# Attention of two pairs ahead of their feed-forward parts, the first pair's token factors put by in DRAM

## The chip, the cores and the metric

The kernel runs on one core of one Trainium2 chip. The metric is the device time of one execution in microseconds, which is shown as the median of several runs. Before the change it is 1606.5 us (three runs, 1605.66 to 1609.31).

## What is computed

The input `x` holds 8 sequences of 512 tokens with 512 features, all float32. Cut to what matters, the reference is:

```python
xn = _layernorm(x)
# s: linear attention
q, k, v = xn @ Wq.T + bq, xn @ Wk.T + bk, xn @ Wv.T + bv
kv_sum = cumsum((elu(k) + 1) * v, axis=1)          # over the tokens
s = ((elu(q) + 1) * kv_sum * SCALE) @ Wo.T + bo
# g: gated feed-forward with Hadamard transforms
h = fwht(xn * SU_ug) / SCALE_F
up = h @ W_up.T * (Wscale_ug[:2048] * SCALE_F)     # 2048 hidden features
gate = h @ W_gate.T * (Wscale_ug[2048:] * SCALE_F)
h = fwht(silu(gate) * up * SU_dp) / SCALE_F
g = silu(h @ W_down.T * (Wscale_dp * SCALE_F))
out = x + s * g
```

`fwht` is the normalized Walsh-Hadamard transform over the last axis. The products of tokens with the four attention weights and the three feed-forward weights are nearly all of the arithmetic.

## The kernel before, in words

The 8 sequences are worked on as four pairs, in a loop `for p in range(B // 2)` (line 935). A pair goes through attention (six groups of products: `k`, `v`, `q` for each half `g` of the features, line 529), the output projection (`project_out`, 601), four feed-forward units (`NU = 4`), and a down projection after the second and after the fourth unit (`down`, 703).

Every matrix product is made with seven block products in place of eight, called P1 to P7. For this, tokens and weights are held as seven factors each: four blocks and three sums or differences. The products are added up in four kinds of PSUM bank, `px` (three buffers), `py` (one), `pz` (two), and `t` (two, for transposes and folds). ScalarE copies a bank that has to be kept (`sa`, `sb`, `sc`, line 328), and VectorE adds the copy and another bank to an output block (line 332). TensorE can use a bank again only after it has been read. In attention and in the first pair's gate and up, `group` (306) makes such a product with matmuls of 128x512 (line 316).

The token factors of a pair are one tile `xo` of 128 partitions x 7 x 7 x 256 numbers, in a pool with one buffer (`xop`, line 64). Four of the second seven are needed by attention and by the first pair's gate and up. The other three are for the later pairs' feed-forward, which uses the seven-product scheme on two levels (49 products of 128x256, `hidden_unit` 647 and `block_product` 467, line 475). `inner_tokens` (157) makes them with three VectorE subtractions of 128x1792, and `inner_t3` (163) finishes with one subtraction for each of the seven outer factors.

The first pair differs from the others, since the weights arrive raw. The Hadamard transform is folded into the weights on the chip:

- Gate and up (`folded_w`, 748): four VectorE butterflies (759 to 762), two matmuls with the Hadamard matrix `had` (768), four scaled ScalarE copies (774), four VectorE sums that make the weight factors (`encode_weights`, 175). `inner_w` (253) then makes and stores the factors of the second level in DRAM, for the later pairs.
- Down (four column blocks `o`): `load_down` (788) brings 1 MB, `butterflies_down` (793) makes one scaling (795) and eight VectorE butterflies of 128x1024 (745, 746), `fold_down` (802) four matmuls (806), sixteen scaled ScalarE copies (812) and a store to `wd_f` (815). `down_w` (241) loads rows of `wd_f` into a `t8` buffer, makes weight factors on VectorE, and stores them.
- The projection weights' factors are made on GpSimd (835) and kept in DRAM (`keep_w`, 189).

The down weights' steps are set in time by a plan, which counts finished groups of products (`between`, 929) and gives the steps a priority of 150 behind what is current (`background`, 75):

```python
for o, (n, a, b) in enumerate(((0, 0, 2), (2, 4, 6), (4, 6, 8), (6, 8, 10))):   # load, butterflies, fold
for n, u, j in ((10, 0, 0), (10, 0, 1), (11, 1, 0), (11, 1, 1), (16, 2, 0), (17, 2, 1), (18, 3, 0), (19, 3, 1)):   # down_w
```

All weights pass through one list, `queue` (845). `get_w` (873) asks for the next three and sets the steps that make them; their loads go to SyncE's DMA queue (SP) in that order. The order of products within and across groups is an agenda (`at`, `advance`, 283 to 300). A scheduler then places all instructions on their engines by dependence and priority. Each engine works through its own list in order, so that an instruction that waits holds up all that stand behind it on its engine.

Other lines that are needed below: `load_x` (105), `layernorm` (116) and `transposed` (137) bring a sequence in. The two sequences of the next pair come through a pool with one buffer (`xin`, 67). In attention, ScalarE and VectorE make elu + 1 (549 to 551), GpSimd multiplies `v` by it (563), VectorE sums over the tokens with scans (565), and the context `co` is made by VectorE (573) and GpSimd (`encode_tokens`, 168). The hidden factors `ho` are made on GpSimd from gate and up (637 to 640). `put_by` and `fetch` (587, 592) keep the attention result `s_` and the first half `d_` of the down projection in DRAM; the second down projection fetches them and `x` again as `y` (976 to 981), and finishes with silu on ScalarE (710), a product on GpSimd (712), a sum on VectorE (713) and the store of the output (716).

The pools in SBUF: `hop` has two buffers of 28 KB a partition, which hold the raw `x` of the first two sequences, `co`, `ho`, and at first the down weights' work tile `rd` (917). `t8` has six of 8 KB, `wpool` four weights, `snap` six.

Of the kernel before, what the change touches and what calls it, by code (L numbers as in the profile page):

```python
# [21 lines left out]
def kernel(  # L22
# [41 lines left out]
    xop = ctx.enter_context(tc.tile_pool(name="xop", bufs=1))  # L64
    hop = ctx.enter_context(tc.tile_pool(name="hop", bufs=2))
# [70 lines left out]

    def transposed(b, xt, xo):
# [15 lines left out]
        if s == 1:  # L153
            o = xo[:, :, 0:4]
            nc.vector.tensor_tensor(o[:, P4], o[:, P2], o[:, P6], ALU.subtract)

    def inner_tokens(xo):

        nc.vector.tensor_tensor(xo[:, :, P5], xo[:, :, P7], xo[:, :, P1], ALU.subtract)
        nc.vector.tensor_tensor(xo[:, :, P6], xo[:, :, P3], xo[:, :, P5], ALU.subtract)  # L160
        nc.vector.tensor_tensor(xo[:, :, P4], xo[:, :, P2], xo[:, :, P6], ALU.subtract)

    def inner_t3(xo, factors):
        for i in factors:
            nc.vector.tensor_tensor(xo[:, i, P7], xo[:, i, P3], xo[:, i, P7], ALU.subtract)

# [300 lines left out]
    def block_product(name, w, x, out, add, done):  # L467
# [5 lines left out]
        def product(p, i, first):  # L473
            for lane in range(2):
                nc.tensor.matmul(  # L475
                    p[:, lane], w[:, lane, i, :], x[:, i, :],
# [52 lines left out]
    def attention(p, xo, get_w):  # L529
        co = hop.tile([P, 2, 7, L], F32, tag="h", name=f"co_{p}")  # L530

        def project(m, g, then):
# [11 lines left out]
            )  # L544

# [101 lines left out]
    def hidden_unit(p, u, xo, ho, get_w, last):  # L647
# [4 lines left out]
        def outer(i, out, add=None, done=None):  # L652
            w = get_w("gu", (u, i))
            block_product(f"gu_{p}_{u}_{i}", w, xo[:, i], out, add, done)
# [87 lines left out]
    def butterfly(eng, dst, src, h):  # L742
        s = src.rearrange("p (a t h) e -> p a t (h e)", t=2, h=h)
        d = dst.rearrange("p (a t h) e -> p a t (h e)", t=2, h=h)
# [42 lines left out]

    def load_down(o, rs):
        r = rs[:, o % 2]
# [3 lines left out]
    def butterflies_down(o, rs):  # L793
        r, r2 = rs[:, o % 2], rs[:, 2]
        nc.vector.tensor_tensor(r, r, wsc_r.unsqueeze(1).to_broadcast([P, NF, P]), ALU.mult)
        butterfly(nc.vector, r2, r, 8)
        butterfly(nc.vector, r, r2, 4)
        butterfly(nc.vector, r2, r, 2)
        butterfly(nc.vector, r, r2, 1)
# [46 lines left out]
    for p in range(B // 2):  # L846
        queue += [(p, m, g) for g in range(2) for m in ("k", "v", "q")]
        for u in range(NU):
            if p == 0:
                queue += [(p, m, f) for m in ("gate", "up") for f in (u, u + NU)]  # L850
            else:
                queue += [(p, "gu", (u, i)) for i in (P1, P5, P6, P2, P7, P3, P4)]
            if u == 0:
                at_o = len(queue) - (2 if p == 0 else 0)
                queue[at_o:at_o] = [(p, "o", 0), (p, "o", 1)]
            if u % 2:
                queue += [(p, "down", (u // 2, i)) for i in (P1, P7, P2, P6, P5, P3, P4)]
    ahead = []

    def ask(n):  # L860
        while queue and len(ahead) < n:
            p, m, g = queue.pop(0)
            w, steps = (first_w if p == 0 and m != "down" else later_w)(m, g)
# [9 lines left out]
    def get_w(m, g):  # L873
# [15 lines left out]
    xs = [  # L889
        load_x(b, hop.tile([P, 2, 7, D], F32, tag="h", name=f"x_{b}")[:, 0, :NT], parts=2)  # L890
        for b in range(2)
    ]
# [12 lines left out]
    xo = xop.tile([P, 7, 7, H], F32, tag="xo", name="xo_0")  # L905
    for b in range(2):
        layernorm(b, xs[b], parts=2)
        transposed(b, xs[b], xo)
# [8 lines left out]
    rs = hop.tile([P, 3, NF, P], F32, tag="h", name="rd")  # L917
    rd = {}
    groups = [0]

    plan = {}
    for o, (n, a, b) in enumerate(((0, 0, 2), (2, 4, 6), (4, 6, 8), (6, 8, 10))):
        plan.setdefault(n, []).append(lambda o=o: load_down(o, rs))
        plan.setdefault(a, []).append(lambda o=o: rd.update({o: butterflies_down(o, rs)}))
        plan.setdefault(b, []).insert(0, lambda o=o: fold_down(o, rd[o]))
    for n, u, j in ((10, 0, 0), (10, 0, 1), (11, 1, 0), (11, 1, 1), (16, 2, 0), (17, 2, 1), (18, 3, 0), (19, 3, 1)):
# [8 lines left out]
    for p in range(B // 2):  # L935
        if p:
            with background():
                inner_tokens(xo)
        co = attention(p, xo, get_w)
# [93 lines left out]
```

## Time and profile before

| | |
|---|---|
| median of three runs | 1606.5 us |
| the profiled execution | 1606.13 us |
| its span in the profile | 1604.3 us |
| granted TensorE clock | 0.992 |
| TensorE matmul (PE) busy | 1550.9 us, 97%, 5936 instructions |
| TensorE weight load (PEld) busy | 1117.1 us, 70% |
| VectorE (DVE) busy | 949.2 us, 59%, 1335 instructions |
| ScalarE (ACT) busy | 425.1 us, 26%, 679 instructions |
| GpSimd (POOL) busy | 504.9 us, 31%, 286 instructions |
| moved by DMA | 254.29 MB, 159 GB/s in the mean |
| chain of work that ended last | TensorE 73%, VectorE 12%, DMA 5%, "issue" 4%, GpSimd 3%, ScalarE 2% |

The page has more parts: the span in 40 equal slices of 40 us, each with the busy share of every engine in tenths; groups of instructions by source line; and the chain of work that ended last. The trace behind it can be asked for an engine's timeline, in which each row has the start, the length, the engine, the line, the operation with its output and inputs by the program's names, the shape of the tiles, and in square brackets the idle time of the engine before the row with the engine and the instruction that ended it. It can also be asked for tables of windows, with the busy time of each engine in a stretch and the number of instructions that make it up. Matmuls overlap, so that a busy TensorE can still be a slow one: the distance between the starts of equal matmuls tells its pace.

### The profile page before, as it was taken

What the parts mean: (1) busy time and instruction counts of PE and PEld (TensorE: products, weight loads), DVE (VectorE), ACT (ScalarE), POOL (GpSimd) and SP (SyncE); (2) the same over time, 40 slices, a digit from 0 to 9 for tenths busy, and PEclk for the clock granted to TensorE, in tenths of its full rate; (3) what the DMA queues carried; (4) which work ended last, traced back from release to release, by engine and by line L of the source; (5) the groups of instructions that cost most, each with busy time, mean ns of one, the idle gap of its engine ahead of it and who ended that gap; (6) DMA issues with size and microseconds to landing.
All of it is one profiled execution on the core that took longest, in us unless ns stands there. A gap on an engine that the chain in (4) does not pass through costs nothing.

```text
span 1604.3 us, 15681 instructions
## 1 busy us (share of the span) xinstructions
PE 1550.9 (97%) x5936; PEld 1117.1 (70%) x5936; DVE 949.2 (59%) x1335; ACT 425.1 (26%) x679; POOL 504.9 (31%) x286
## 2 busy tenths in 40 slices
PE   6979989999999999999999999999999999999998
PEld 3335435854485478888886478888887468888887
DVE  6869666268565574715675475634675466542673
ACT  3333322132324431111222531111221441111211
POOL 4531342103322235302622236201622137120731
PEclk9999999999999999999999999999999999999999
DMA  8234559397763244335574232535474224525472
GB/s 266 80 111 135 180 148 300 84 280 215 250 218 129 69 138 145 131 107 189 178 255 144 90 107 102 193 91 188 158 265 157 69 93 137 176 83 190 141 261 84
DMA packets 147723, 254.29 MB, mean 159 GB/s; under 512 B 7232, under 2 KB 109120, under 8 KB 143552
## 3 DMA queue, kind: packets, MB, share of 16 engines
q1 hardware_dynamic: 147360, 253.00, 47.9%
q8 instruction: 47, 0.77, 0.2%
q10 hardware_dynamic: 288, 0.30, 0.1%
q14 instruction: 28, 0.23, 0.0%
HBM read 183.53 MB, written 69.73 MB: 158 GB/s over the span
## 4 chain that ended last, share of the span: by engine, by line
PE 73%; DVE 12%; DMA 5%; issue 4%; POOL 3%; ACT 2%; SPq 1%; POOLq 0%; DVEq 0%; ACTq 0%
PE px_gu L475 18%; PE pz_gu L475 9%; PE px_dn L391 8%; PE py_gu L475 5%; PE pz_dn L391 4%; PE px_o L391 3%; PE px_v L316 3%; PE px_k L316 3%; PE px_q L316 3%; PE py_dn L391 2%; DMA x<-in_x_dram 2%; POOL s L712 2%; PE pz_o L391 2%; PE pz_q L316 2%; PE pz_k L316 1%
## 5 line engine op out<-in xcount | busy, mean ns | idle before, releaser
L475 PE MATMUL px_gu<-xo,w_gu 128*128 128x256 f32 x1344 | 320.6, 380 | 0.0
L475 PEld LDWEIGHTS px_gu<-xo,w_gu 128*128 128x128 f32 x1344 | 254.7, 190 | 39.9 <-issue 3.6
L391 PE MATMUL px_dn<-w_down,ho 128*128 128x256 f32 x1024 | 230.1, 379 | 2.2 <-DVE sb_dn L402 1.7
L391 PEld LDWEIGHTS px_dn<-w_down,ho 128*128 128x128 f32 x1024 | 193.6, 190 | 31.4 <-DVE sb_dn L402 2.7
L475 PE MATMUL pz_gu<-xo,w_gu 128*128 128x256 f32 x672 | 173.1, 380 | 0.0
L675 POOL TENSOR_TENSOR u<-u,v 128x1024 f32<-128x1024 f32 x24 | 56.1, 2360 | 354.2 <-DVE u L513 354.2
L475 PEld LDWEIGHTS pz_gu<-xo,w_gu 128*128 128x128 f32 x672 | 127.0, 190 | 19.1 <-DVE a L517 0.9
L391 PE MATMUL pz_dn<-w_down,ho 128*128 128x256 f32 x512 | 116.6, 380 | 1.9 <-POOL ho L172 1.9
L391 PEld LDWEIGHTS pz_dn<-w_down,ho 128*128 128x128 f32 x512 | 96.4, 190 | 17.6 <-POOL ho L172 2.7
L712 POOL TENSOR_TENSOR s<-s,d 128x512 f32<-128x512 f32 x30 | 43.0, 1435 | 166.2 <-ACT d L710 166.2
L475 PE MATMUL py_gu<-xo,w_gu 128*128 128x256 f32 x336 | 86.2, 379 | 0.0
L563 POOL TENSOR_TENSOR v<-v,k 128x1024 f32<-128x1024 f32 x16 | 39.8, 2486 | 138.5 <-ACT v L538 110.3
L637 POOL TENSOR_TENSOR ho<-g,u 128x512 f32<-128x512 f32 x8 | 17.8, 2224 | 186.0 <-DVE u L332 186.0
L475 PEld LDWEIGHTS py_gu<-xo,w_gu 128*128 128x128 f32 x336 | 63.9, 190 | 8.7
L316 PE MATMUL px_k<-xo,w_k 128*128 128x512 f32 x128 | 63.0, 616 | 3.7 <-ACT sa_k L328 3.4
L316 PE MATMUL px_up<-xo,w_up 128*128 128x512 f32 x128 | 60.4, 600 | 4.0 <-DVE w_up L178 4.0
L679 POOL TENSOR_TENSOR v<-v,r 128x1024 f32<-128x1024 f32 x24 | 56.2, 2364 | 25.6 <-DVE r L513 25.6
L316 PE MATMUL px_v<-xo,w_v 128*128 128x512 f32 x128 | 60.2, 593 | 3.5 <-ACT sc_v L328 3.5
L316 PE MATMUL px_q<-xo,w_q 128*128 128x512 f32 x128 | 60.2, 593 | 0.0
L316 PE MATMUL px_gate<-xo,w_gate 128*128 128x512 f32 x128 | 59.6, 593 | 0.0
L565 DVE TENSOR_TENSOR_SCAN k<-ones,v 128x512 f32<-128x512 f32 x32 | 39.4, 1271 | 33.5 <-POOL v L563 33.5
L391 PE MATMUL py_dn<-w_down,ho 128*128 128x256 f32 x256 | 58.0, 379 | 0.0
(241 smaller groups left out, 2469.0 us busy)
## 6 DMA issues: line engine op xcount, KB each, us to landing
w_gu<-d_gu SPq DMA_DIRECT2D x84, 896.0 KB, 4.5
w_down<-d_down SPq DMA_DIRECT2D x56, 512.0 KB, 3.6
d_s<-o SPq DMA_DIRECT2D x8, 1024.0 KB, 4.4
d_d<-dn SPq DMA_DIRECT2D x8, 1024.0 KB, 7.5
d<-d_d SPq DMA_DIRECT2D x8, 1024.0 KB, 6.2
s<-d_s SPq DMA_DIRECT2D x8, 1024.0 KB, 7.3
y<-in_x_dram SPq DMA_DIRECT2D x8, 1024.0 KB, 8.4
out_dram<-y SPq DMA_DIRECT2D x16, 512.0 KB, 3.1
```

Of the source, the lines that this page charges most:

```text
L316: nc.tensor.matmul(p.rearrange("p a t -> p (a t)") if len(r.shape) == 2 else p, ws[k][:, i, :], r, start=(first and k == 0), stop=(k == n ...
L391: nc.tensor.matmul(p[:, c], t[:, (2 * g + c) * P : (2 * g + c + 1) * P], ws[i](k), start=(first and k == 0 and c == 0), stop=(k == n - 1), ...
L475: nc.tensor.matmul(p[:, lane], w[:, lane, i, :], x[:, i, :], start=(first and lane == 0), stop=True, skip_group_check=True,)
L563: nc.gpsimd.tensor_tensor(v[:, h], v[:, h], k[:, h], ALU.mult)
L565: nc.vector.tensor_tensor_scan(k[:, h, s], ones.to_broadcast([P, L]), v[:, h, s], 0.0, ALU.mult, ALU.add)
L637: nc.gpsimd.tensor_tensor(ho[:, P1], g[:, 0, 0], r[:, 0, 0], ALU.mult)
L675: nc.gpsimd.tensor_tensor(r[:, m], ru1[:, m], rv[:, m], ALU.add)
L679: nc.gpsimd.tensor_tensor(rv[:, m], rv[:, m], rr[:, m], ALU.add)
L712: (nc.vector if last else nc.gpsimd).tensor_tensor(r, r, d, ALU.mult)
```

## The change

Pair 0's attention is followed by pair 1's attention. Then comes pair 1's feed-forward, then pair 0's. Pairs 2 and 3 run as before, each with its attention and its feed-forward.

- Token factors: the tile `xo` is split into `xo` (7 x 4 x 256, pool `xop`) and `xi` (the three inner ones, 7 x 3 x 256, new pool `xip` with one buffer). Pair 0's `x0` lies in a `hop` buffer; the raw `x` of sequences 0 and 1 lie in `t8` buffers.
- During pair 0's attention, after its first and third group, sequences 2 and 3 are loaded, normalized and transposed into pair 1's `x1`, with a priority of 40 behind what is current. After its second group, `put_x0` writes `x0` (128 x 7168 numbers, 3.67 MB) to DRAM.
- Pair 0's output projection runs after the first group of pair 1's attention; its weights stand there in the queue.
- Pair 1's feed-forward is now the one with raw weights. After its last unit, `fetch_x0` reads the 3.67 MB back into `xo` and makes the inner factors in `xi`. Pair 0's feed-forward uses the stored weight factors, as those of pairs 2 and 3.
- The down weights' work tile lies where `xi` will be. It holds two and a half column blocks in place of three, so that the butterflies run over halves of 64 columns: sixteen of half the size, in place of eight, for each block. The rearrangement in `butterfly` keeps two axes apart for that.
- The plan's numbers are set anew, since twelve groups of attention and the output projection now stand ahead of the first gate. Folds are put at the end of their step's list in place of its front.

The instructions of attention, feed-forward and down projection are otherwise those of before. The core of the diff:

```diff
+    xip = ctx.enter_context(tc.tile_pool(name="xip", bufs=1))
...
+    def new_x(p, pool):
+        return pool.tile([P, 7, 4, H], F32, tag="h" if pool is hop else "xo", name=f"xo_{p}")
+
+    def new_inner(p):
+        return xip.tile([P, 7, 3, H], F32, tag="xi", name=f"xi_{p}")
...
-    def inner_tokens(xo):
-
-        nc.vector.tensor_tensor(xo[:, :, P5], xo[:, :, P7], xo[:, :, P1], ALU.subtract)
-        nc.vector.tensor_tensor(xo[:, :, P6], xo[:, :, P3], xo[:, :, P5], ALU.subtract)
-        nc.vector.tensor_tensor(xo[:, :, P4], xo[:, :, P2], xo[:, :, P6], ALU.subtract)
+    def inner_tokens(xo, xi):
+
+        nc.vector.tensor_tensor(xi[:, :, P5 - P4], xo[:, :, P7], xo[:, :, P1], ALU.subtract)
+        nc.vector.tensor_tensor(xi[:, :, P6 - P4], xo[:, :, P3], xi[:, :, P5 - P4], ALU.subtract)
+        nc.vector.tensor_tensor(xi[:, :, 0], xo[:, :, P2], xi[:, :, P6 - P4], ALU.subtract)
...
+    def inner_factor(xo, xi, i):
+        return lambda k: xo[:, i, k] if k < P4 else xi[:, i, k - P4]
...
-    def attention(p, xo, get_w):
+    def attention(p, xo, get_w, behind):
+
+        n = iter(range(6))
...
+            behind.get(next(n), lambda: None)()
...
     def butterfly(eng, dst, src, h):
-        s = src.rearrange("p (a t h) e -> p a t (h e)", t=2, h=h)
-        d = dst.rearrange("p (a t h) e -> p a t (h e)", t=2, h=h)
+        s = src.rearrange("p (a t h) e -> p a t h e", t=2, h=h)
+        d = dst.rearrange("p (a t h) e -> p a t h e", t=2, h=h)
...
+    def down_tiles(rs):
+        n = NF * P
+        r = [rs[:, i * n : (i + 1) * n].rearrange("p (c e) -> p c e", c=NF) for i in range(2)]
+        return r + [rs[:, 2 * n : 2 * n + n // 2].rearrange("p (c e) -> p c e", c=NF)]
...
     def butterflies_down(o, rs):
-        r, r2 = rs[:, o % 2], rs[:, 2]
+        r, r2 = rs[o % 2], rs[2]
         nc.vector.tensor_tensor(r, r, wsc_r.unsqueeze(1).to_broadcast([P, NF, P]), ALU.mult)
-        butterfly(nc.vector, r2, r, 8)
-        butterfly(nc.vector, r, r2, 4)
-        butterfly(nc.vector, r2, r, 2)
-        butterfly(nc.vector, r, r2, 1)
+        for e in range(2):
+            half = r[:, :, e * P // 2 : (e + 1) * P // 2]
+            butterfly(nc.vector, r2, half, 8)
+            butterfly(nc.vector, half, r2, 4)
+            butterfly(nc.vector, r2, half, 2)
+            butterfly(nc.vector, half, r2, 1)
         return r
...
+    list_attention(True, 0)
+    list_attention(False, 1, [("o", 0), ("o", 1)])
+    queue[7:9] = [(True, "o", 0), (True, "o", 1)]
+    list_ffn(True, False, True)
+    list_ffn(False, False, False)
+    for p in range(2, B // 2):
+        list_attention(False, p)
+        list_ffn(False, False, True)
...
-    xs = [
-        load_x(b, hop.tile([P, 2, 7, D], F32, tag="h", name=f"x_{b}")[:, 0, :NT], parts=2)
-        for b in range(2)
-    ]
+    xs = [load_x(b, t8.tile([P, NT, D], F32, tag="t", name=f"x_{b}"), parts=2) for b in range(2)]
...
-    xo = xop.tile([P, 7, 7, H], F32, tag="xo", name="xo_0")
+    x0 = new_x(0, hop)
...
-    rs = hop.tile([P, 3, NF, P], F32, tag="h", name="rd")
+    rs = down_tiles(xip.tile([P, 7 * 3 * H], F32, tag="xi", name="rd"))
...
-    for o, (n, a, b) in enumerate(((0, 0, 2), (2, 4, 6), (4, 6, 8), (6, 8, 10))):
+    for o, (n, a, b) in enumerate(((0, 1, 3), (3, 5, 7), (6, 8, 10), (9, 11, 13))):
         plan.setdefault(n, []).append(lambda o=o: load_down(o, rs))
         plan.setdefault(a, []).append(lambda o=o: rd.update({o: butterflies_down(o, rs)}))
-        plan.setdefault(b, []).insert(0, lambda o=o: fold_down(o, rd[o]))
-    for n, u, j in ((10, 0, 0), (10, 0, 1), (11, 1, 0), (11, 1, 1), (16, 2, 0), (17, 2, 1), (18, 3, 0), (19, 3, 1)):
+        plan.setdefault(b, []).append(lambda o=o: fold_down(o, rd[o]))
+    for n, u, j in ((14, 0, 0), (15, 0, 1), (15, 1, 0), (16, 1, 1), (22, 2, 0), (23, 2, 1), (24, 3, 0), (25, 3, 1)):
         plan.setdefault(n, []).append(lambda u=u, j=j: down_w(u, j))
...
+    def tokens(b, xo):
+        t = load_x(b)
+        layernorm(b, t)
+        transposed(b, t, xo)
...
+    def load_next(p):
+        held["x"] = [load_x(2 * p + s) for s in range(2)]
+        for s in range(2):
+            layernorm(2 * p + s, held["x"][s])
+
+    def transpose_next(p):
+        held["xo"] = new_x(p, xop)
+        for s in range(2):
+            transposed(2 * p + s, held["x"][s], held["xo"])
...
+    def put_x0():
+        nc.sync.dma_start(d_x0, x0.rearrange("p i k t -> p (i k t)"))
+
+    def fetch_x0():
+        held["xo"] = xo = new_x(0, xop)
+        nc.sync.dma_start(xo.rearrange("p i k t -> p (i k t)"), d_x0)
+        held["xi"] = xi = new_inner(0)
+        with background():
+            inner_tokens(xo, xi)
+            inner_t3(xo, range(7))
+
+    x1 = new_x(1, xop)
+
+    def next_tokens(b):
+        with background(40):
+            tokens(b, x1)
+
+    co0 = attention(0, x0, get_w, {0: lambda: next_tokens(2), 1: put_x0, 2: lambda: next_tokens(3)})
+    co1 = attention(1, x1, get_w, {0: lambda: project_out(0, co0, get_w)})
+    ffn(1, x1, None, True, co1, {3: fetch_x0})
+    ffn(0, held["xo"], held["xi"], False, None, {2: lambda: load_next(2), 3: lambda: transpose_next(2)})
+    for p in range(2, B // 2):
+        xo, xi = held["xo"], new_inner(p)
+        with background():
+            inner_tokens(xo, xi)
+        co = attention(p, xo, get_w, {})
+        inner_t3(xo, (P1, P5, P6, P2, P7))
+        at(9, lambda: inner_t3(xo, (P3, P4)))
...
```

`ffn` holds what the loop over the pairs held (line 935 on): the four units, the output projection after the gates or after the first unit if there is one to do, the two down projections, and after each unit the step that it is given in `after`.

## The prediction

> **What bounds the kernel now.** I read the page's slices first, then TensorE's timeline for its gaps, then VectorE's timeline at those gaps. In the slices (40 us each, busy tenths) PE is short of 9 only in the first 240 us and near 480 us:
>
> ```profile
> PE   6979989999999999999999999999999999999998
> DVE  6869666268565574715675475634675466542673
> ```
>
> Busy PE is not PE at its peak, so I use its pace. In the timeline eight 128x512 records take 3.43 us and the 80 `px_dn` records of 128x256 take 17.27 us, so 0.429 and 0.216 us each. The later pairs run at that pace: their first `px_k` stand at 497.8, 868.9 and 1237.8 us, 369 to 371 us apart, and their records (168 x 0.429 for attention, 784 + 112 + 448 at 0.216 for the rest) make 362 us, with transposes some 366. The first pair takes 479 us from 18.4 to 497.8 us. Its records are 168 + 448 + 96 of 128x512 (attention, gate and up, folds), 305 us, and 560 of 128x256, 121 us, with transposes about 432: some 45 us are lost, and only there can this change gain. TensorE's timeline shows where; the bracket is the idle time before the row and what ended it:
>
> ```profile
> 63.27 3.00 PE L316 MATMUL pz_q<-xo,w_q 128*128 128x512 f32 x4 [3.55 <-DVE q L332]
> ...
> 89.84 1.96 PE L316 MATMUL px_v<-xo,w_v 128*128 128x512 f32 x4 [3.52 <-ACT sc_v L328]
> ...
> 106.66 3.78 PE L316 MATMUL pz_q<-xo,w_q 128*128 128x512 f32 x4 [4.32 <-DVE q L332]
> ...
> 150.74 2.00 PE L391 MATMUL pz_o<-w_o,co 128*128 128x256 f32 x8 [3.05 <-DVE g L332]
> ...
> 202.96 2.69 PE L316 MATMUL px_up<-xo,w_up 128*128 128x512 f32 x4 [4.02 <-DVE w_up L178]
> ...
> 228.34 3.47 PE L316 MATMUL pz_gate<-xo,w_gate 128*128 128x512 f32 x4 [3.62 <-DVE g L332]
> ...
> 497.77 3.58 PE L316 MATMUL px_k<-xo,w_k 128*128 128x512 f32 x4 [2.28 <-ACT sa_k L328]
> ```
>
> Four such rows usually take 1.88 us. After a gap[...] they take more, here and in the next row: 1.9 us at 63, 2.7 at 107, 1.8 at 203, 1.6 at 228. So the six waits of 63 to 228 us cost 5.4 + 3.5 + 7.0 + 3.1 + 5.8 + 5.2 = 30 us, and one of 1.3 us at 235 makes 31.3. VectorE's timeline shows what stands in front of the awaited result:
>
> ```profile
> 57.69 3.33 DVE L565 TENSOR_TENSOR_SCAN k<-ones,v 128x512 f32<-128x512 f32 x2 [2.24 <-POOL v L563]
> 60.94 1.68 DVE L745 TENSOR_TENSOR rd<-rd 128x1024 f32<-128x1024 f32 x1
> 62.54 0.67 DVE L332 TENSOR_TENSOR q<-sc_q,pz_q 128x512 f32<-128x512 f32 x1
> ```
>
> The 0.67 us sum that TensorE waits for lies behind two scans, which wait for POOL, and behind a down-weight butterfly. The windows say the same: VectorE is full at 60 to 100 us, and in the second pair's attention it isn't:
>
> ```profile
> 60.00:80.00 20.00, 16.49 (x34) 7.06 (x35) 20.00 (x18) 8.18 (x10) 7.88 (x5) 0.91 0.22 75
> ...
> 540.00:560.00 20.00, 20.00 (x48) 8.76 (x47) 10.04 (x12) 9.95 (x13) 6.20 (x5) 1.00 0.20 73
> ```
>
> (Columns: stretch, length, PE, PEld, DVE, ACT, POOL busy, clock, DMA share, GB/s.)
>
> [...]That is what the two windows show: one VectorE-bound, one with VectorE half idle. [...]the butterflies' median is 1220 ns, but 1393 (L745) and 1533 ns (L746) in the mean, longest where POOL works.
>
> **The change, part by part.**
>
> *Work.* Pair 1 takes over the raw gate and up products, pair 0 the stored seven-factor ones; records, folds and transposes only change places. TensorE's sum stays the same: 0 us.
>
> *Butterflies.* 32 instructions of 1024 elements become 64 of 512. [...]the trace has 1220 and 690. Started back to back they take 1.13 and 0.60 us in the timeline: 64 x 0.60 - 32 x 1.13 = +2.2 us of VectorE, up to +5 if the start isn't hidden. I take 0 on the path, as one pair's attention has some 40 us of free VectorE; without that cover it is 2 to 5 us. Shorter pieces also hold a waiting sum for less: up to -0.6 us a wait.
>
> *VectorE in the first attention.* It loses one set of butterflies and the gate folds (2.3 + 9.1 and about 5 us) and, by the built program's order, gets the layernorm and evacuation of sequences 2 and 3: 8 BN_STATS at 0.65, 8 scalings at 0.6, 12 subtractions at 0.4, one of 1.3 us, small ones: about 18 us. So the first attention is hardly lighter. The second has 37 us of its own and the output projection's 16 x 0.6 = 10, against 96 us of TensorE, and takes 2.5 butterfly sets at 12 us: 77 of 96 us. In the first feed-forward unit one set is left instead of two. So I count the waits at 63, 90, 107, 203, 228 and 235 us as gone (28 us) and keep 3 us for the one at 151.
>
> *New wait 1, transposes.* In the built order TensorE has sequence 2's transposes after the first half of the second `k` group, at 53.6 us on the old clock. They wait for VectorE: after the first scan (50.3, set by POOL's product) come statistics (2 us), a sum, three scans to about 59 us (POOL's second product takes from 54 to 57), then the scaling: 60 us. So 6.5 us, and 1.8 for the restart: 8 us; from 5[...] to 15 (loads late). Sequence 3 has one buffer with it and starts loading at about 63 us; its transposes come at 86: 1 us, up to 4.
>
> *Storing pair 0's factors.* 128 x 7168 x 4 B is 3.67 MB, put on SP's queue at about 27 us, in front of `w_v` (issued at 37.4 us in the old trace) and sequence 2's load. [...]the trace's best windows move 325 to 346 GB/s, so 11 to 13 us. It ends at about 40 us, as `w_v` is issued, and replaces 2 MB of down weights there. I take 0; at 200 GB/s it costs 6 us, which is in the 15 above. Hidden by attention's TensorE work.
>
> *New wait 2, output projection.* It now stands in the second pair's first `k`, with 20 half butterflies among its sums. VectorE reaches the last `co` product about 118 us when TensorE wants it at 114: 4 us, between 0 and 7. Three fold sets before the first gate leave TensorE waiting for ScalarE's scaled copies: four copies take 1.14 us against 0.43 of matmul, two banks: 2 us (0 to 4).
>
> *New wait 3, down weights.* Their encoding is asked for two to three groups earlier, its loads waiting on SP for a POOL-held `t8` buffer and standing on VectorE in front of `u`'s sums: 3 us, between 0 and 9.
>
> *The joint between the feed-forwards.* Old: 2.3 us at 497.8 with 1.7 us of restart, and some 2.5 us of small waits before. New: the 3.67 MB come back after the last up product of pair 1 (447 us on the old clock) and land some 13 us later; on SP `y` twice (2 MB) and then the fourth `w_down` stand behind. At 340 GB/s that weight lands 20 us after the up, and TensorE wants it after 16: 4 us and 1.7 of restart; with half a dozen small waits 7 us, so 0.5 more than before. Bounds: 0 and 18.
>
> **Sum.** Gone 28. New: 8 + 1 + 4 + 2 + 3 + 0.5 = 18.5. Net -9.5 us on the profiled execution's 1606.13 us (span 1604.3, 1.8 around it), which lies 0.4 under the median of 1606.5: 1597 us.
>
> **Rivals.**
> - B, new waits stay small. For it: the later pairs' attentions run the same products and scans without loss, once no butterflies stand between them. Against it: the first attention has layernorms there instead. The waits 1 to 3 then cost 8 instead of 18: 1587 us.
> - C, VectorE stays the limit: what is taken from one place is paid at another, as VectorE has the same work to do before the second feed-forward unit, only spread over 96 us more of TensorE. For it: the new waits 1 to 3 are all VectorE's; at two thirds of the way to their upper ends they make up for what went. Gone 28, new 27: 1605 us.
> - D, slower, by the fetch of pair 0's factors. VectorE runs in order; its seven-factor subtractions (3 x 2.0 us and 7 x 0.4 to 0.7) stand in front of the down sums that free TensorE's banks. If the fetch lands 13 us after the last up they end in time within 2 us. Each later microsecond is one of TensorE. It is slower than before once it lands 26 us after, as when the 2 MB of `y`, the 1 MB of `x` and the rest of `d` and `s` (3 MB) share the engines: 9.7 MB at 340 GB/s is 29 us, 1612 us with the restart. Against it: `d`, `s` and `x` are issued 12 us earlier.
> - That the change doesn't do what it says can't be: the built order has both attentions ahead of the first gate.
>
> **How the numbers follow.** Forecast 0.48 (1591 to 1602), B 0.20 (1580 to 1591), C 0.15 (1602 to 1609), D 0.17 (over 1609). A measurement of this kernel tells about 0.2%, 3.2 us, from no change. Faster by more: most of the forecast and B, a little of C, 0.70; within: 0.13; slower: 0.17. The range leaves out the lower third of B and two thirds of D: 1583 to 1612.
>
> **What would show it.** Right: no wait of 3 us on `pz_q` before the first gate, one of 5 to 9 us before sequence 2's transposes ended by VectorE's scaling, VectorE below 18 of 20 us in all windows of the second attention, no wait for `w_up`'s encoding in the first unit. Wrong: `px_dn` or `w_down` waits of over 8 us in pair 1's second down; waits for `u` or `w_gate` sums in the first unit above 8 us together; or transposes that don't wait at all.

## The result, and the profile after

The changed kernel takes 1607.99 us in the median (12 runs, 1602.70 to 1612.04), the kernel before 1605.69 us beside it (12 runs). The ratio is 1.0014 with a 95% interval of 0.9999 to 1.0028: no change that can be told, +2.2 us on 1605.7 where -9.5 was forecast. The profiled execution of the changed kernel took 1603.91 us (span 1602.1), one of the shorter ones of its kernel, and that of before 1606.13. So the two traces differ by 2 us the other way: they are used here for the places where time is lost, not for how much the kernels differ. The median execution of the changed kernel is 4 us longer than the profiled one, and no trace places these 4 us.

First the page's slices of the changed kernel, 40 us each, busy tenths:

```profile
PE   6888999899999999999999999999999999999998
DVE  5697867672576446715675575634675466542673
```

PE is short of 9 in the first four slices and at 280 to 320 us. The short slice of before at 200 to 240 us has filled up and the third has risen from 7 to 8, but the second and the fourth have sunk from 9 to 8, and VectorE has a 9 at 80 to 120 us. TensorE's timeline has the places (in brackets the idle time before the row, and what ended it):

```profile
59.29 1.99 PE L149 MATMUL pt<-ident,x 128*128 128x128 f32 x8 [6.23 <-DVE x L130]
...
94.17 1.29 PE L149 MATMUL pt<-ident,x 128*128 128x128 f32 x8 [1.61 <-DVE xo L159]
...
111.74 1.99 PE L326 MATMUL pz_q<-xo,w_q 128*128 128x512 f32 x4 [1.68 <-DVE q L342]
...
123.07 4.90 PE L401 MATMUL px_o<-w_o,co 128*128 128x256 f32 x12 [5.05 <-DVE co L586]
...
133.29 1.35 PE L401 MATMUL pz_o<-w_o,co 128*128 128x256 f32 x4 [1.88 <-POOL co L182]
...
317.46 2.85 PE L781 MATMUL pw_gate<-r_gate,had 128*128 128x512 f32 x4 [4.02 <-DVE r_gate L775]
...
559.94 15.34 PE L401 MATMUL px_dn<-w_down,ho 128*128 128x256 f32 x62 [2.38 <-DMA w_down<-d_down]
```

Of the six waits of before, four are gone, the one for `g` at 151 us is left with 0.7 us (at 263 us), and the one for `pz_q` at 107 us with 1.7 us, at 112 us. Six others have come. To add them up I take, from the timeline, the distance from the start of each matmul to that of the next, less the usual distance of its kind (0.429 us for 128x512, 0.216 for 128x256, 0.109 for a transpose); this counts the slow rows after a gap too. Lost are:

| stretch | before | after |
|---|---|---|
| first attention to the second unit's gate | 37.7 us (40 to 240) | 24.6 (40 to 140), 0.0 (140 to 220), 5.3 (220 to 300), 8.1 (300 to 340): 38.0 us |
| to the end of the joint | 8.4 us (280 to 300, 420 to 520) | 5.3 us (540 to 600) |
| later joints | 5.3 us | 7.1 us |

The first line is the case: 38 us were lost up to the second unit's gate, and 38 us are lost now. The windows tell which engine was full (columns as before: stretch, length, PE, PEld, DVE, ACT, POOL busy, clock, DMA share, GB/s). First two of the kernel before,

```profile
80.00:100.00 20.00, 16.46 (x38) 6.87 (x37) 19.96 (x20) 5.78 (x9) 6.40 (x3) 1.00 0.20 53
100.00:120.00 20.00, 15.31 (x29) 6.01 (x28) 7.56 (x10) 8.11 (x23) 9.63 (x9) 0.83 0.46 163
```

then three of the changed kernel:

```profile
80.00:100.00 20.00, 17.41 (x51) 7.83 (x50) 20.00 (x29) 11.29 (x16) 9.54 (x7) 1.00 0.21 77
100.00:120.00 20.00, 16.34 (x40) 7.14 (x38) 19.93 (x21) 4.75 (x6) 8.13 (x5) 1.00 0.35 117
120.00:140.00 20.00, 15.04 (x43) 10.48 (x44) 17.68 (x21) 7.49 (x8) 6.59 (x4) 0.74 0.14 46
```

VectorE is full from 80 to 120 us, where it was full from 60 to 100. VectorE's timeline of the changed kernel shows what stands ahead of the context `co` that the output projection waits for at 123 us:

```profile
117.65 0.69 DVE L758 TENSOR_TENSOR rd<-rd 128x512 f32<-128x512 f32 x1
118.26 0.68 DVE L759 TENSOR_TENSOR rd<-rd 128x512 f32<-128x512 f32 x1
118.86 1.22 DVE L564 SCALAR_TENSOR_TENSOR q<-q,neg_q 128x1024 f32<-128x1024 f32 x1
120.00 0.69 DVE L758 TENSOR_TENSOR rd<-rd 128x512 f32<-128x512 f32 x1
120.60 0.68 DVE L759 TENSOR_TENSOR rd<-rd 128x512 f32<-128x512 f32 x1
121.20 0.68 DVE L342 TENSOR_TENSOR q<-sb_q,pz_q 128x512 f32<-128x512 f32 x1
121.80 1.22 DVE L586 SCALAR_TENSOR_TENSOR co<-k,q 128x1024 f32<-128x1024 f32 x1
```

It is the picture of before at 60 us: half butterflies between the steps of an awaited sum, without a gap. The wait at 317 us has another queue. In VectorE's timeline the encoding of two down-weight blocks stands in front of the last step of a gate weight:

```profile
307.99 0.68 DVE L774 TENSOR_TENSOR r_gate<-r_gate 128x512 f32<-128x512 f32 x1
308.59 3.98 DVE L187 TENSOR_TENSOR wd<-wd 128x256 f32<-128x256 f32 x2
312.49 2.88 DVE L188 TENSOR_TENSOR wd<-wd 128x256 f32<-128x256 f32 x2
...
316.64 0.68 DVE L775 TENSOR_TENSOR r_gate<-r_gate 128x512 f32<-128x512 f32 x1
```

and GpSimd's timeline has, in the same 7 us, four instructions on `ho` without a gap:

```profile
308.22 2.66 POOL L652 TENSOR_TENSOR ho<-g,u 128x1024 f32<-128x1024 f32 x1 [3.89 <-DVE u L342]
310.96 1.33 POOL L180 TENSOR_TENSOR ho<-ho 128x512 f32<-128x512 f32 x1
312.25 1.44 POOL L182 TENSOR_TENSOR ho<-ho 128x512 f32<-128x512 f32 x1
313.65 1.44 POOL L181 TENSOR_TENSOR ho<-ho 128x512 f32<-128x512 f32 x1
```

Four sums of 0.41 us (the length of their like at 315 us) take 6.9 us: 2.57, 1.48, 1.48 and 1.48 us, beside GpSimd instructions of 2.66, 1.33, 1.44 and 1.44 us. The first sum behind GpSimd's last instruction takes 0.41 us again.

### The profile page after: what moved, and what is told of

Read it like the earlier page. It is cut to its first block, busy times and chain, and to the rows that moved or that the text cites. A ratio compares the mean times of both kernels' runs of the same rounds, so it can differ in the third digit from the quotient of the medians.

```text
span 1602.1 us, 15724 instructions
## 1 busy us (share of the span) xinstructions
PE 1548.5 (97%) x5936; PEld 1117.9 (70%) x5936; DVE 958.5 (60%) x1367; ACT 425.8 (27%) x679; POOL 496.1 (31%) x286
## 4 chain that ended last, share of the span: by engine, by line
PE 80%; DVE 9%; DMA 3%; POOL 2%; ACT 2%; issue 2%; SPq 1%; POOLq 0%; ACTq 0%; DVEq 0%
PE px_gu L485 18%; PE px_dn L401 9%; PE pz_gu L485 9%; PE py_gu L485 4%; PE pz_dn L401 4%; PE px_gate L326 3%; PE px_o L401 3%; PE px_q L326 3%; PE px_v L326 3%; PE px_up L326 3%; PE px_k L326 3%; PE py_dn L401 2%; POOL s L725 2%; DMA w_down<-d_down 2%; DMA x<-in_x_dram 2%
## 5 line engine op out<-in xcount | busy, mean ns | idle before, releaser
L485 PE MATMUL px_gu<-xi,w_gu 128*128 128x256 f32 x672 | 173.8, 380 | 0.2 <-ACT sa_gu L493 0.2
L485 PE MATMUL px_gu<-xo,w_gu 128*128 128x256 f32 x672 | 172.1, 379 | 0.0
L485 PEld LDWEIGHTS px_gu<-xi,w_gu 128*128 128x128 f32 x672 | 126.9, 190 | 20.9 <-issue 1.4
L485 PEld LDWEIGHTS px_gu<-xo,w_gu 128*128 128x128 f32 x672 | 127.7, 190 | 18.2 <-issue 1.0
L485 PE MATMUL pz_gu<-xi,w_gu 128*128 128x256 f32 x336 | 86.5, 380 | 0.0
L485 PE MATMUL pz_gu<-xo,w_gu 128*128 128x256 f32 x336 | 86.4, 380 | 0.0
L485 PEld LDWEIGHTS pz_gu<-xi,w_gu 128*128 128x128 f32 x336 | 63.4, 190 | 9.6 <-DVE u L516 0.8
L485 PEld LDWEIGHTS pz_gu<-xo,w_gu 128*128 128x128 f32 x336 | 63.7, 190 | 9.2 <-DVE a L527 0.6
L650 POOL TENSOR_TENSOR ho<-g,u 128x512 f32<-128x512 f32 x8 | 11.3, 1410 | 177.6 <-DVE u L342 177.6
L401 PE MATMUL px_o<-w_o,co 128*128 128x256 f32 x256 | 60.9, 389 | 5.3 <-DVE co L586 5.1
```

Source lines behind the costliest of these rows:

```text
L401: nc.tensor.matmul(p[:, c], t[:, (2 * g + c) * P : (2 * g + c + 1) * P], ws[i](k), start=(first and k == 0 and c == 0), stop=(k == n - 1), ...
L485: nc.tensor.matmul(p[:, lane], w[:, lane, i, :], x(i), start=(first and lane == 0), stop=True, skip_group_check=True,)
L650: nc.gpsimd.tensor_tensor(ho[:, P1], g[:, 0, 0], r[:, 0, 0], ALU.mult)
```

## The experiments

My theory after the result was rival C with a place: VectorE has as much to do before the first gate as before, its butterflies come in dense rows, and wherever they stand, a sum that TensorE waits for stands behind them. Rivals: the new waits are each their own matter (transposes at the wrong place in TensorE's order, the context's chain too long, tokens loaded late behind the 3.67 MB), so that each can be taken away and stays away.

**What the butterflies cost in each kernel.** The four butterfly steps are left out of `butterflies_down`, so that the hidden axis' Hadamard transform is incomplete; all else stays.

```diff
-        butterfly(nc.vector, r2, r, 8)
-        butterfly(nc.vector, r, r2, 4)
-        butterfly(nc.vector, r2, r, 2)
-        butterfly(nc.vector, r, r2, 1)
```

> The kernel before without the 32 butterflies of the down weights (so the Hadamard transform of the hidden axis is incomplete; loads, scaling, folds and stores stay). If the six waits between 63 and 235 us are VectorE's queue behind butterflies, about 25 to 30 us go: 1576 to 1581 us. If the awaited sums are late for another reason[...], less than 12 us go: over 1594 us.

Measured: 1582.73 us, ratio to the kernel before 0.9866 (0.9853 to 0.9880), 21.5 us less. A little under the forecast: four of the six waits go, two stay in part, one of 2.5 us behind the scans and this one, in TensorE's timeline,

```profile
204.38 3.78 PE L316 MATMUL pz_gate<-xo,w_gate 128*128 128x512 f32 x4 [3.52 <-DVE g L332]
```

which stands behind the four steps of an up weight, three of which take 1.6 to 1.8 us each where the first takes 0.69. The same steps of the kernel before take 1.66, 1.75 and 1.64 us at 222 to 227 us, with GpSimd's `ho` instructions of 1.27, 1.72 and 1.71 us beside them. So the 228 us wait of before, 5.2 us in my sum, was not the down butterflies' alone.

In the changed kernel the loop over the two halves is taken out in the same way.

> The changed kernel without its 64 half butterflies (the same part of the computation is left out). If VectorE stayed the limit and the waits only moved to other places (rival C), they go here too, but for the 8 us of sequence 2's transposes and the encoding of the down weights: 14 to 20 us less than the changed kernel, 1588 to 1594 us. If the new waits are the chain's own length (context factors late for the output projection even on a free VectorE), less than 8 us go: over 1600 us.

Measured: 1593.00 us, ratio 0.9931 (0.9918 to 0.9944). Against the changed kernel's 1.0014 that is 13.3 us. The waits at 112, 123 and 133 us are gone; those of the transposes and of the gate weight stand as they were:

```profile
59.30 1.98 PE L149 MATMUL pt<-ident,x 128*128 128x128 f32 x8 [6.13 <-DVE x L130]
...
302.91 3.75 PE L781 MATMUL pw_gate<-r_gate,had 128*128 128x512 f32 x4 [4.02 <-DVE r_gate L775]
```

So the change took 8 us off the price of the butterflies (21.5 to 13.3), not the 24 that the forecast has (28 gone, 4 new). And without any butterflies the changed kernel is 10 us slower than the one before: it brought a cost of its own.

**What the layernorms cost.** `layernorm(b, t)` is left out of `tokens`, so that the raw tokens of sequences 2 and 3 are used.

> The changed kernel without the layernorm of sequences 2 and 3 for pair 1's attention and feed-forward (their raw tokens are transposed). If the waits of the transposes (59, 87 and 94 us, 11 us with restarts) are VectorE's statistics and scalings, they go, and the context is ready earlier too: 1592 to 1598 us. If the tokens' loads are late, behind the 3.67 MB of pair 0's factors on the queue, the wait at 59 us stays above 3 us: 1602 us or more.

Measured: 1597.68 us, ratio 0.9946 (0.9925 to 0.9967), 10.9 us less than the changed kernel. TensorE's timeline now has

```profile
78.11 0.63 PE L149 MATMUL pt<-ident,x 128*128 128x128 f32 x4 [1.68 <-DVE xo L159]
...
105.59 3.78 PE L326 MATMUL pz_q<-xo,w_q 128*128 128x512 f32 x4 [4.54 <-DVE q L342]
```

The transposes wait 1.7 us once, so the loads were in time. But the matmul behind the q sum waits 4.5 us: the first butterflies now run from 73 us, in place of 84, and what VectorE is freed of is partly taken by them.

> Neither the down weights' butterflies nor the layernorm of sequences 2 and 3 (both parts are left out). If the butterflies and the layernorms ahead of the first gate are the account, this comes to the kernel before without butterflies, 1582.7 us, within 3 us: 1581 to 1586 us. If the encoding of the down weights and the joint between the feed-forwards hold a share of their own, it stays above 1587 us.

Measured: 1583.92 us, ratio 0.9861 (0.9842 to 0.9881). The account closes: with both gone the changed kernel is where the one before is without butterflies (0.9866; the intervals overlap). Layernorms: 0.9931 to 0.9861, 11.2 us. In the kernel before, the same layernorms run at 436 to 466 us, at the end of pair 0's feed-forward. No run takes them out there; in TensorE's timeline the first sequence's transposes wait for them for less than a microsecond, the second's not at all:

```profile
441.09 1.11 PE L142 MATMUL pt<-ident,x 128*128 128x128 f32 x8 [0.73 <-DVE x L129]
```

The encoding and the joint have no net share that the times would show: their waits (4 us each, at 294 and 540 us) stand against those that are left in the kernel before without butterflies (the 3.5 us above, 2.3 us at the joint and smaller ones).

**What the halves cost.** The kernel before with the halves of 64 columns; all three blocks of its work tile stay.

```diff
-        butterfly(nc.vector, r2, r, 8)
...
+        for e in range(2):
+            half, part = r[:, :, e * P // 2 : (e + 1) * P // 2], r2[:, :, : P // 2]
+            butterfly(nc.vector, part, half, 8)
...
```

> The kernel before with its butterflies in halves of 64 columns, as in the changed kernel. If the shorter pieces hold the awaited sums less, 1 to 3 us go: 1602 to 1604 us. If VectorE is full where they run, each set costs 0.6 us more[...]: 2 to 6 us more, 1607 to 1611 us. Forecast of the prediction for the path: 0.

Measured: 1609.70 us, ratio 1.0028 (1.0017 to 1.0040), 4.5 us more. The groups by line say why. Before:

```profile
L746 DVE TENSOR_TENSOR rd<-rd 128x1024 f32<-128x1024 f32 x16 | 24.5, 1533 | 0.0
...
L745 DVE TENSOR_TENSOR rd<-rd 128x1024 f32<-128x1024 f32 x16 | 22.3, 1393 | 0.1
```

With halves, in the same kernel:

```profile
L745 DVE TENSOR_TENSOR rd<-rd 128x512 f32<-128x512 f32 x32 | 28.5, 889 | 0.5
L746 DVE TENSOR_TENSOR rd<-rd 128x512 f32<-128x512 f32 x32 | 28.2, 880 | 0.0
```

Busy time 46.8 to 56.7 us. About half of that is the instructions' own length (64 x 0.69 us against 32 x 1.22 us, 5 us). The other half is what they take beyond it, 12.5 us in place of 7.8: the halves of line 745 have a median of 0.69 us, and the longest takes 2.73. Of the 32 whole ones 9 are more than 15% longer than 1.22 us, up to 3.37, and each of these has a GpSimd instruction beside it. In the changed kernel the busy time is 54.2 us, +7.4. I had +2.2 to +5, and 0 on the path. That share wasn't measured in the changed kernel itself: three whole blocks (24 KB a partition) don't fit into the place of `xi` (21 KB).

**Moving single steps.** Pair 0's output projection one group later:

```diff
-    co1 = attention(1, x1, get_w, {0: lambda: project_out(0, co0, get_w)})
+    co1 = attention(1, x1, get_w, {1: lambda: project_out(0, co0, get_w)})
```

(with its weights one place later in the queue).

> The output projection of pair 0 stands behind the second group of pair 1's attention in place of the first. If it was asked for too early, its two waits for the context (123 and 133 us, 11 us with the restarts) go and nothing takes their place: 1597 us. If VectorE has more work there than TensorE has time, the waits turn up at the next sums of pair 1's attention (k and v), and at most 4 us go: 1604 us or more.

Measured: 1611.34 us, ratio 1.0047 (1.0035 to 1.0059), slower. The waits turn up behind k, v and q of pair 1: 2.9 us at 123, 2.8 at 150, 4.4 at 227.

The second to fourth set of butterflies later in the plan:

```diff
-(0, 1, 3), (3, 5, 7), (6, 8, 10), (9, 11, 13)
+(0, 1, 3), (3, 7, 9), (7, 9, 11), (10, 12, 14)
```

> The second set of butterflies two groups later (the third and fourth one group later). If the 12 halves in front of the last q sum and of the context make the output projection late, 6 to 9 us go: 1599 to 1602 us, and the wait at 123 us falls under 2 us. If the chain itself is late, the waits stay and nothing goes: 1606 to 1610 us.

Measured: 1613.00 us, ratio 1.0055 (1.0042 to 1.0068). This tells nothing of the theories at 123 us: the halves stand at the same times to 0.3 us up to 178 us. The scheduler seems to fill VectorE with background steps as soon as their data are there; the later place in the program didn't move them. Only the fourth set moved (232 to 246 us), and waits of 2.4 and 2.9 us came up at 221 and 269 us.

So I tied them: from the second half of the first set on, a copy of one column of the context into the work tile has to come first. The first set's fold comes five groups later for it, and the later sets' butterflies and folds one to three.

```diff
+            if o == 0 and e == 1:
+                yield
+                nc.vector.tensor_copy(r2[:, 0, 0:1], co0[:, 1, P3, 0:1])
             half = r[:, :, e * P // 2 : (e + 1) * P // 2]
```

> From the second half of the first set on, no butterfly can start before the last context product of pair 0: a one-column copy of the context is written into the butterflies' work tile first. (The later sets also load and fold one or two groups later.) If the halves in front of the last q sum and the context make the output projection late, its two waits (7.3 us, 11.5 with restarts) fall under 3 us together; as the sets now reach into the first gates, up to the same is given back there: 1598 to 1608 us in all. If the chain of scans, elu and GpSimd's sums is late by itself, the two waits stay above 6 us.

Measured: 1621.98 us, ratio 1.0107 (1.0094 to 1.0120). In its timeline of TensorE:

```profile
120.25 2.86 PE L401 MATMUL px_o<-w_o,co 128*128 128x256 f32 x12 [0.59 <-DVE co L586]
...
127.51 1.13 PE L401 MATMUL pz_o<-w_o,co 128*128 128x256 f32 x4 [1.82 <-POOL co L182]
...
253.30 3.75 PE L830 MATMUL pwd<-rd,had 128*128 128x512 f32 x4 [16.45 <-DVE rd L759]
```

The wait of 5.05 us for the context is down to 0.59: it was the halves in front of it, not its own chain. The wait behind it stays (1.88 to 1.82 us). And the sets are then late for their folds, 16 us.

The down weights' encoding later, at the distance that it had in the kernel before:

```diff
-(14, 0, 0), (15, 0, 1), (15, 1, 0), (16, 1, 1), (22, 2, 0), (23, 2, 1), (24, 3, 0), (25, 3, 1)
+(17, 0, 0), (17, 0, 1), (18, 1, 0), (18, 1, 1), (23, 2, 0), (24, 2, 1), (25, 3, 0), (26, 3, 1)
```

> The encoding of the down weights is asked for two to three groups later for the first half, one for the second, so that its sums leave the place in front of the butterflies of the next gate weight. If the wait of 4.2 us at 317 us (with restarts and two smaller ones 9 us) is the queue behind these eight sums while GpSimd makes ho, it falls under 1.5 us and 5 to 9 us go: 1599 to 1603 us. If the butterflies of that gate weight are late for their own load, the wait stays: 1606 to 1610 us.

Measured: 1604.96 us, ratio 1.0009 (1.0000 to 1.0018). The wait at 317 us is gone, and one of 3.5 us stands at 345 us, for a ScalarE copy that is late behind a g sum, and this behind other VectorE work. From the changed kernel's 1.0014 that is 0.8 us, and the intervals don't part.

Tokens of sequences 2 and 3 one group later each:

```diff
-{0: lambda: next_tokens(2), 1: put_x0, 2: lambda: next_tokens(3)}
+{1: lambda: (put_x0(), next_tokens(2)), 3: lambda: next_tokens(3)}
```

> Sequences 2 and 3 are brought in behind the second and fourth group in place of the first and third. If the 8 us at 59 us is only a matter of the place of the transposes in TensorE's order, it shrinks to under 4 us, and 3 to 6 us go: 1602 to 1605 us. If VectorE has no room for the layernorms anywhere in the first attention, other sums are late for as much: 1607 to 1612 us.

Measured: 1613.69 us, ratio 1.0059 (1.0041 to 1.0077). The wait at 61 us is 1.8 us, and others come up: 4.4 us at 91, 3.2 at 110, 5.3 at 131.

**Moving TensorE's order alone.** Sequence 2's transposes 40 behind in priority:

```diff
         layernorm(b, t)
-        transposed(b, t, xo)
+        with background(40 if b == 2 else 0):
+            transposed(b, t, xo)
```

> Only sequence 2's transposes stand 40 further behind in priority, so that TensorE has some 7 us of products before them; VectorE's order is the same. If the 8 us at 59 us are lost by the place of the transposes alone, they fall under 1.5 us and 5 to 8 us go: 1600 to 1603 us. If VectorE's backlog sets the pace of the first attention, the same time is lost at the next sums: under 2 us go, 1606 us or more.

Measured: 1603.51 us, ratio 0.9984 (0.9974 to 0.9995): some 5 us less than the changed kernel, and a little under the one before. The 6.2 us at 59 us are gone: products that stood behind the waiting transposes run there now, from 52 to 60 us. In their place TensorE's timeline has

```profile
61.82 2.57 PE L326 MATMUL pz_q<-xo,w_q 128*128 128x512 f32 x4 [1.95 <-DVE q L342]
...
91.88 1.97 PE L149 MATMUL pt<-ident,x 128*128 128x128 f32 x8 [5.76 <-DVE x L130]
```

Sequences 2 and 3 share one buffer: it comes free later, the load goes at 71 in place of 64 us, and sequence 3's transposes are the ones that wait.

With the later encoding as well:

> The later transposes and the later encoding of the down weights together. If the two are separate waits on TensorE's path, the gains add: 1597 to 1601 us, faster than both kernels. If both only move their waits, it is 1604 us or more.

Measured: 1601.49 us, ratio 0.9974 (0.9964 to 0.9983): 4 us under the kernel before and 6 us under the changed one. The later encoding's share, 0.9984 to 0.9974, is 1.6 us, and these two intervals overlap.

Then, on top of that, both sequences' transposes later (`background(40)` for both):

> As the run with later transposes and later down-weight encoding, but with sequence 3's transposes 40 further behind too. If their wait of 6.2 us at 91 us is again only their place in TensorE's order, it goes and 4 to 8 us go with it: 1594 to 1598 us. If VectorE is simply full from 80 to 120 us, so that sequence 3's factors and the first context end when they end, the time turns up at pair 1's first k or at the output projection: 1600 us or more.

Measured: 1602.17 us, ratio 0.9986 (0.9978 to 0.9994), no gain. Waits of 6.1 and 3.7 us at 92 and 107 us, fewer at the output projection.

Or a buffer of its own for sequence 3:

```diff
-        t = load_x(b)
+        t = load_x(b, t8.tile([P, NT, D], F32, tag="t", name=f"x_{b}") if b == 3 else None)
```

> As the run with later transposes of sequence 2 and later down-weight encoding (1601.5 us), but sequence 3's raw tokens have a buffer of their own, so that their load goes 10 to 15 us earlier, by 55 us in place of 71. There the wait moved from sequence 2 to sequence 3 (6.2 us at 91 us, 9 with the restart), since both use one buffer. If that buffer is the link, this wait falls under 2 us and 5 to 9 us go: 1593 to 1597 us. If VectorE's load up to 120 us sets the time, as in the run with both transposes later, the wait turns up at a q sum or at the context: 1600 us or more.

Measured: 1599.97 us, ratio 0.9964 (0.9950 to 0.9977), the fastest version here. The load goes at 51 us and the transposes' wait falls to 2.7 us, but the q sum at 111 us now waits 3.2 us: of the 9 us in question some 1.6 are gained (0.9974 to 0.9964), and the intervals overlap.

**Whether the second attention could have hidden the butterflies.** The tie again, on top of later transposes (sequence 2) and later encoding, with the later sets nearer to their old places.

> As the run with later transposes (sequence 2 alone) and later down-weight encoding, but the half butterflies from the second half of the first set on stand behind the last context product of pair 0, with the later sets shifted by one or two groups. If only the order was at fault and VectorE has room in the second attention, the waits of the output projection (5.7 us with two smaller ones, 7.9 with restarts) fall under 4 us and nothing comes back: 1596 to 1599 us. If the four sets can't be done before the folds in time, a wait at the folds before or after the first gate gives it back: 1602 us or more.

Measured: 1616.64 us, ratio 1.0061 (1.0041 to 1.0081). VectorE is busy for 10 of 20 us from 140 to 180, since the third block's load waits for the first block's fold, which stands at 200 us; then a fold waits 20.1 us. So the folds of the first two sets were taken out of the background:

```diff
+    def fold_now(o):
+        with background(-150 if o < 2 else 0):
+            fold_down(o, rd[o])
```

> As the second tied run (butterflies behind pair 0's context, later transposes, later down-weight encoding), with one more change: the folds of the first two sets are no longer 150 behind in priority, so that TensorE takes them as soon as their butterflies are done, and the buffers come free for the next two loads. In the run before this one VectorE was half idle from 147 to 219 us, since the third load waited for the first fold. If the second attention has room for the butterflies and only buffers and order were at fault, the 20 us wait at 234 us and those of the output projection are both gone: 1594 to 1599 us, faster than the run without the tie (1601.5). If VectorE's load sets the pace there, waits of pair 1's v, q and k sums come up between 140 and 220 us: 1602 us or more.

Measured: 1612.41 us, ratio 1.0051 (1.0035 to 1.0066). The 20 us are gone, and still nothing is gained. The windows of this run:

```profile
140.00:160.00 20.00, 20.00 (x64) 11.99 (x64) 9.11 (x16) 6.17 (x19) 0.00 (x0) 1.00 0.52 197
160.00:180.00 20.00, 20.00 (x48) 8.93 (x47) 11.92 (x10) 8.16 (x23) 5.09 (x2) 1.00 0.68 209
180.00:200.00 20.00, 17.01 (x36) 7.03 (x35) 19.89 (x26) 9.40 (x12) 4.46 (x2) 0.91 0.26 77
200.00:220.00 20.00, 18.02 (x39) 7.64 (x38) 19.97 (x23) 5.33 (x9) 6.11 (x4) 0.91 0.22 68
```

and the row that follows them in TensorE's timeline:

```profile
228.80 3.78 PE L326 MATMUL pz_q<-xo,w_q 128*128 128x512 f32 x4 [6.15 <-DVE q L342]
```

VectorE is half idle for 40 us, then full for 40, and the matmuls behind the sums of v and q wait. The free time that I counted is there, but in none of the three tied runs did the third and fourth block get into it. The work tile holds two whole blocks, so the third block's load goes after the first block's fold and store (at 164 us here), and its steps on VectorE start at 172 us, those of the fourth at 197. Other ways, such as a larger work tile, weren't run.

## Why the prediction was wrong

The step that failed is the one that has the butterflies at 0 on the path, and with it the 28 us "counted as gone" at full value. By this step 24 us were to go (28, less the 4 us of the output projection); the removals show that 8 went, 21.5 us before and 13.3 us after. The rest stands in the order of the prediction.

- **The reading of the page.** It has no slice short of 9 near 480 us; the wait at 498 us is in the timeline alone. And from how long a gap on the rows behind it are slow doesn't come out of the lines: the one at 498 us has a gap of 2.3 us and a slow row (3.58 us), the one at 90 us a gap of 3.5 us and a row of nearly the usual length (1.96 us).
- **Waits at 63 to 235 us, 28 us gone.** They went, but for 1.7 us. But the butterflies, taken away, cost 21.5 us there (19 to 24), not 28; part of the 107 us and 228 us waits had a second cause. That of the 228 us wait, VectorE's steps beside GpSimd's `ho`, is met again at 317 us in the changed kernel.
- **Butterflies, 0 on the path; free time in the second attention.** 13.3 us stay on the path. I compared sums (77 of 96 us of VectorE). That a sum fits into a stretch says nothing on the instruction that waits in it: VectorE was full from 80 to 120 us, where the first context is made, and busy for 13.5 to 18.6 of 20 us from 140 to 220. My own remark that the first attention is "hardly lighter" should have decided: VectorE's busy time from 40 to 120 us is 62.5 us before and 67.4 us after. The halves alone cost 4.5 us in the kernel before; I had named 2 to 5 us as their price without the cover.
- **New wait 1, transposes, 8 and 1 us.** Right in place, size and cause: 6.2 us of idle time and 8.0 with the slow rows at 59 us, some 3 for sequence 3, and 11 us by removal of the layernorms. The scans and the statistics of my chain stand ahead of the scaling in VectorE's timeline. But some 5 us went when the transposes alone were moved in TensorE's order, so their place there has a share beside VectorE's load.
- **Storing pair 0's factors, 0.** Right: it landed after 9.8 us, where I had 11 to 13 (the best windows of before, 325 to 346 GB/s, make 10.6 to 11.3), and the transposes don't wait for the load.
- **New wait 2, output projection, 4 us (0 to 7).** Mis-sized: 5.1 and 1.9 us of idle time, some 11 with the slow rows. The halves ahead of `co` made the first of the two, as the tied run shows; the second goes when the butterflies are left out, but not with this tie. I had counted the sums and not the halves that are dealt between them. The folds before the first gate, 2 us (0 to 4), were right: 1.7 us from 220 to 240 us.
- **New wait 3, down weights, 3 us (0 to 9).** 8.1 us in the trace, within its bounds; beside GpSimd's `ho` instructions four sums of 0.41 us took 6.9. Taking it away gave 1 to 2 us, inside the intervals.
- **The joint, 0.5 us more.** 1.3 us less in the traces (6.6 us from 420 to 520 us before, 5.3 after), and 1.8 us less at the first down projection. The factors came back 12.3 us after their issue, and the weight behind them was 2.4 us late, where I had 4. Rival D is out.
- **The sum.** Forecast: butterflies -24, layernorms +9, the rest +5.5, in all -9.5. Measured: butterflies 21.5 to 13.3, layernorms 0 (by the trace alone) to 11.2, the rest -0.8, in all +2.2 us. Rival C, at 0.15, named what the removals show: what was taken from one place is paid at another, 21.5 us before and 24.5 now.
- **The signs.** No sign of "wrong" came, and three of the four of "right" did (the q waits, 6.2 us at the transposes, no wait for `w_up`). The fourth failed: VectorE was busy for 18.6 of 20 us at 160 to 180 us. The signs looked at the old waits and at the transposes, none at the output projection, where 11 us were lost.

Open: how the 13.3 us divide between the halves' greater length and their place, and how much of the gain of later transposes is lost again to VectorE's load and how much to the shared buffer; the runs part them only to a microsecond or two.

## What to carry to other kernels

Spreading an engine's work over a longer stretch helps only if the pieces can lie where the engine is idle. Look at what ties them (work tiles, loads behind folds, a scheduler that fills at once) and count what can stand before an awaited result, not the busy share of the stretch. Name signs for the new places too, or they can come true while the time doesn't. When a step is moved out of a cover, as the layernorms here, its price can turn up in the new place. And splitting instructions to save room added to their length here (64 x 0.69 us against 32 x 1.22), and what they took beyond it grew as well, from 7.8 to 12.5 us.

## What the runs showed of the hardware

Two sizes are worth keeping. The first is what VectorE loses beside GpSimd. Sums of 128x256 that take 0.41 us alone took 1.48 to 2.57 us each. Of the 64 halves in the changed kernel, the 47 with no GpSimd instruction beside them took at most 0.69 us; ten of the other 17 took longer, up to 2.84 us, so that the means are 864 and 832 ns.

The second is what two gaps of TensorE in a short time cost. The waits of 5.1 and 1.9 us at 123 and 133 us cost some 11 us in all: behind the first, 128x256 matmuls started 0.43 us apart in place of 0.22, until 127 us, and the granted clock is 0.74 over these 20 us. The rows after the gap of 4.3 us in the kernel before were slow for as long (107 to 112 us, the clock 0.83 over 20 us).
